# Cross-attention with layer norm: a new written order for the last ten tiles, head halves kept together, and three small changes at the end

## The chip, the core and the metric

The kernel runs on one core of one Trainium2 chip. The core has a matrix engine (TensorE, PE in the profile; its weight loads are the row PEld), a vector engine (VectorE, DVE), an activation engine (ScalarE, ACT), a general engine (GpSimd, POOL) and a queue engine (SyncE, SP). Each works through its own instructions in order; they meet by semaphores. DMA transfers are issued from SP, ACT or POOL and move data between the device memory (HBM), the on-chip buffer (SBUF) and within SBUF. Matmul results land in eight banks of an accumulation memory (PSUM) of 512 fp32 columns each. The metric is device time in microseconds (us), the median of several runs.

## The reference

There are 4 batches of 2048 rows of x, each row 512 wide, and 4 contexts of 77 rows. What is computed:

```python
qs = (x @ wq)                     # 16 heads of 32
ks, vs = ctx @ wk, ctx @ wv
scores = einsum(qs, ks) / sqrt(32)
scores = where(mask, -inf, scores)    # mask over the 77 keys
attn = softmax(scores) @ vs           # per head
out = attn @ wo + x
mu, var = mean(out), mean((out - mu)**2)   # over the 512 columns
return (out - mu) / sqrt(var + 1e-5) * gamma + beta
```

All inputs and outputs are fp32.

## The kernel before, in words

The 8192 rows are 64 tiles of 128 rows, numbered 0 to 63. Two tiles are a block (0 to 31), four a group that shares one load of x transposed, 16 a batch. To keep precision at the fast matmul rate, the big products (q projection, output projection) split each operand into a rounded high part and a low rest (both fp32r) and add three products: high by high, low by high, high by low. That is 12 matmuls of 128x128 weights and 512 columns for a projection of a tile.

One tile goes through these steps; the letters are the words in which the last ten tiles' order is written:

- `Q` / `q` (lines 173 to 189): a quarter of a group's q projection on TensorE, and its copy to SBUF by VectorE.
- `S` (L302): 64 small score matmuls into four banks, one for each head index j within groups of four.
- `T54.2` (L316): for quarter 2 of tile 54 (the four heads of one bank), VectorE adds the mask, writes the scores to a buffer `pbuf`, and finds the row maxima (negated). This frees the bank.
- `e` (L330): ScalarE's exponentials of a quarter, with row sums.
- `r`, `n` (L341, L346): VectorE's reciprocal of the 16 sums, then GpSimd's normalisation of the whole tile. For tile 63 alone, `h63.0`, `m63.0` and `h63.1`, `m63.1` do it in two halves (L354, L360).
- `t` (L370): VectorE transposes the tile in 32x32 blocks into buffer B.
- `P26.7s` (L382): piece 7 of the 12 DMAs which regroup block 26's transposed tiles into the tile PT; the last letter is the issuing queue (s SP, g POOL, a ACT). `U62.7s` is the same for a single tile, used for 62 and 63.
- `V` / `W` (L400, L415): attention times values, for a block (two banks) or for one of the last two tiles. `a`, `b` (or `c`, `d` for single tiles; L431, L435): ScalarE and VectorE split the result into high part AH and low part AL.
- `O` (L466): the output projection, 12 matmuls; in the last ten tiles the four that need AL come last. `x` loads the rows of x; `+` (L469) adds them on VectorE. `X` (L453) instead opens O's bank with the rows of x by one plain fp32 matmul with an identity matrix; then there is no `+`, and the statistics read PSUM.
- `s` (L505, L507): VectorE's mean and variance, or `I`, `J` (L513, L519): ScalarE's mean and squares. `u` (L529 to L532): GpSimd's 1/sqrt(var + eps), two small instructions. 
- `y` and `z` (L555, L558): VectorE's (o - mean) * gamma, then * rstd + beta. Or `k` (ScalarE's scaling, L541) or `p` (GpSimd's, L545), followed by `f`: GpSimd's times gamma, plus beta (L496, L497). `M0` and `M1` copy gamma and beta into two PSUM banks that stay taken, for y and z. `i`, `j`, `v` are a cast and split of x transposed, and a bias for k.
- `w` (L500): the store of the tile, issued on SP.

Tiles 0 to 53 are laid out by the loop at L644, two tiles a turn, with scores of later tiles, projections and norms of earlier ones interleaved. From S54 on (420.5 us in the profile) the order of all remaining work is the text `ORDER`, read word by word: a word puts its instructions at the end of their engines' queues, and every engine keeps that order. PSUM banks are given out in a ring of eight by the same order, so that a word that takes a bank waits for the last reader of what held it before.

Buffer `pbuf` has three slots, B two, PT two: T of tile t waits for t of tile t-3, t of a block for all P of the block two before, P for the V two blocks before.

## Time and profile before

| | us |
|---|---|
| median of 3 runs | 517.16 |
| lowest, highest | 516.73, 517.35 |
| the profiled execution: its time | 516.79 |
| the profiled execution: its span, first to last instruction | 515.0 |
| busy of the span: PE, DVE, ACT, POOL | 503.8, 473.5, 470.3, 418.7 |
| last matmul ends | 507.9 |
| last instruction of VectorE ends | 512.1 |

A timeline row reads: start, length, engine, line, operation, what it writes and from what, shape, how many in a row, and in square brackets how long the engine had been idle and what ended that. Lengths of neighbours overlap, because instructions are pipelined: the step from start to start is the price. The chain rows read start, length, what. A row of waits reads: who waited for whom, us in total, times, longest.

### The profile page before, as it was taken

Reading aid. Unit: us, or ns where it says so; the run is one execution under the profiler, and the core shown is the slowest. Engines: PE = TensorE matmul, PEld = TensorE weight load, DVE = VectorE, ACT = ScalarE, POOL = GpSimd, SP = SyncE. Lnnn points to the kernel's source line nnn. Section 1 sums busy time; section 2 is a strip of 40 time slices with the busy share of each in tenths; the row PEclk is TensorE's granted clock in tenths of the full one; section 3 lists DMA queues with packets and bytes.
Section 4 is the critical chain, followed back from the end, with each engine's and each line's share of the span. In section 5 each row is a group of like instructions: output and inputs, shape, how many; then the busy total and the mean of one; then the engine's idle time right before and its main releaser. Section 6 shows DMA issues by size and latency. Waiting matters only on the chain.

```text
span 515.0 us, 20430 instructions
## 1 busy us (share of the span) xinstructions
PE 503.8 (98%) x6836; PEld 385.2 (75%) x6836; DVE 473.5 (92%) x2572; ACT 470.3 (91%) x2240; POOL 418.7 (81%) x376
## 2 busy tenths in 40 slices
...
GB/s 319 396 138 162 208 187 178 227 200 206 228 214 208 231 211 229 215 205 202 212 206 224 234 218 214 203 198 223 227 193 229 200 207 233 183 222 176 175 210 209
DMA packets 58937, 110.24 MB, mean 214 GB/s; under 512 B 9393, under 2 KB 11313, under 8 KB 58833
## 3 DMA queue, kind: packets, MB, share of 16 engines
...
q8 instruction: 55, 0.90, 0.8%
...
q14 instruction: 50, 0.40, 0.2%
...
## 4 chain that ended last, share of the span: by engine, by line
PE 83%; DMA 5%; POOL 4%; DVE 4%; SPq 2%; issue 1%; ACT 0%; DVEq 0%; POOLq 0%
PE pq L170 30%; PE po L466 29%; PE sc L302 10%; PE pa L400 10%; DMA PT<-B 4%; SPq L382 2%; PE pv L236 2%; DVE B L370 1%; PE pk L196 1%; PE pq L599 1%; POOL mvt L532 1%; DVE pbuf L316 1%; POOL o_end L545 1%; DMA xtf<-xT 1%; POOL o_end L496 1%
## 5 line engine op out<-in xcount | busy, mean ns | idle before, releaser
L330 ACT ACTIVATE pbuf<-pbuf,nm 128x77 f32<-128x77 f32 x1024 | 352.5, 352 | 16.2 <-DVE nm L316 14.8
L330 ACT ACTIVATION_READ_ACCUMULATOR pbuf<-pbuf,nm 128x1 f32 x1024 | 196.9, 192 | 0.0
L316 DVE CUSTOM_DVE_ANT_0 pbuf<-sc,mb 128x77 f32<-128x77 f32 x1024 | 170.7, 230 | 23.3 <-PE sc L302 23.2
L346 POOL TENSOR_TENSOR pbuf<-pbuf,ri 128x1232 f32<-128x1232 f32 x63 | 142.2, 2258 | 22.9 <-DVE ri L341 16.1
L170 PE MATMUL pq<-xth,wqh 128*128 128x512 f32 (+1 forms) x256 | 98.8, 386 | 0.0
L170 PE MATMUL pq<-xtl,wqh 128*128 128x512 f32 (+1 forms) x256 | 97.9, 382 | 0.0
L170 PE MATMUL pq<-xth,wql 128*128 128x512 f32 (+1 forms) x256 | 97.9, 382 | 0.0
L370 DVE STREAM_TRANSPOSE B<-pbuf 128x1280 f32<-128x1280 f32 x64 | 95.5, 1493 | 2.2 <-DMA PT<-B 1.8
L466 PE MATMUL po<-woh,AH 128*128 128x512 f32 x232 | 96.9, 418 | 0.0
L466 PE MATMUL po<-wol,AH 128*128 128x512 f32 x232 | 90.6, 391 | 0.0
L466 PE MATMUL po<-woh,AL 128*128 128x512 f32 x232 | 88.9, 391 | 0.0
L316 DVE DVE_READ_ACCUMULATOR2_ANT nm<- 128x1 f32 x1024 | 84.0, 82 | 0.0
L496 POOL TENSOR_TENSOR o<-o,gam 128x512 f32<-128x512 f32 x50 | 65.6, 1311 | 14.1 <-ACT o L492 14.0
L302 PEld LDWEIGHTS sc<-kct,q 32*64 32x64 f32 x4096 | 51.6, 130 | 24.4 <-issue 23.0
L497 POOL TENSOR_TENSOR o<-o,bet 128x512 f32<-128x512 f32 x50 | 64.5, 1289 | 3.9
L163 POOL TENSOR_TENSOR xtl<-xtf,xth 128x1024 fp32r<-128x1024 f32 x28 | 67.1, 2397 | 0.0
L302 PE MATMUL sc<-kct,q 32*64 32x77 f32 x4096 | 62.1, 237 | 0.7 <-DVE nm L316 0.3
L400 PE MATMUL pa<-PT,vsb 96*32 96x256 f32 x960 | 58.0, 382 | 1.5 <-DMA PT<-B 1.2
L170 PEld LDWEIGHTS pq<-xth,wqh 128*128 128x128 f32 x256 | 48.1, 188 | 9.8
L170 PEld LDWEIGHTS pq<-xth,wql 128*128 128x128 f32 x256 | 48.1, 188 | 9.4
L170 PEld LDWEIGHTS pq<-xtl,wqh 128*128 128x128 f32 x256 | 48.1, 188 | 9.1
L466 PEld LDWEIGHTS po<-woh,AH 128*128 128x128 f32 x232 | 43.5, 187 | 13.0 <-issue 0.7
...
## 6 DMA issues: line engine op xcount, KB each, us to landing
...
```

The costliest lines, as they stand in the source:

```text
L163: nc.gpsimd.tensor_tensor(l, fx.pop((g, c)), h.bitcast(F32), ALU.subtract)
L170: nc.tensor.matmul(pq, w[:, c, m * P : (m + 1) * P], r[:, c, rs], start=(n == 0), stop=(n == 11))
L236: nc.tensor.matmul(pv, ctx_s[c][i][:, r, :], v[c], start=(n == 0), stop=(n == 11))
L302: nc.tensor.matmul(sc[j][half : half + P // 2, g * NK : (g + 1) * NK], qs[q, g, r0 : r0 + P // 2], kct[q, g, t // TPB, keys_of(j)], start= ...
L316: nc.vector.tensor_tensor_reduce(pb[:, h // 2, (h % 2) * NK : (h % 2 + 1) * NK], scs[t][j][:, g * NK : (g + 1) * NK], mb[:, t % TPB, keys_ ...
L330: nc.scalar.activation(pb[:, h // 2, (h % 2) * NK : (h % 2 + 1) * NK], pb[:, h // 2, (h % 2) * NK : (h % 2 + 1) * NK], AF.Exp, bias=nmax[t ...
L346: nc.gpsimd.tensor_tensor(pv, pv, rv.to_broadcast((P, NP, 2, NK)), ALU.mult)
L370: nc.vector.transpose(bt.rearrange("p c q r -> p q c r"), pbuf[t % NPB].rearrange("p q (c r) -> p q c r", c=5),)
L400: nc.tensor.matmul(pas[b, g // 2][HD * j : HD * (j + 1), (g % 2) * BLK : (g % 2 + 1) * BLK], vsb[:, 2 * b // TPB, HD * h : HD * (h + 1)], ...
L466: nc.tensor.matmul(pos[t], a[:, c, rs], w[:, c, :], start=(first and n == 0), stop=(n == 11))
L496: nc.gpsimd.tensor_tensor(o, o, gam, ALU.mult)
L497: nc.gpsimd.tensor_tensor(o, o, bet, ALU.add)
```

## The change

It has five parts.

1. `ORDER` is written anew. Of its 398 words most are the same as before, in another sequence; some issues change their queue, and some tiles change the engines that normalise them: tile 59 and 61 get `x` and `+` in place of `X`; the words p and f now work on tiles 46 to 49, 51 and 53; tiles 55, 58 and 60 get their statistics by I and J; and tiles 52 and 56 are scaled by the words y, K (ScalarE times rstd) and G (GpSimd plus beta).
2. `slot(h)`: in pbuf and all that follows from it, the heads with j = 0, 1 of each group come first (slots 0 to 7), then those with j = 2, 3. Before, both halves alternated in pairs. The half views become plain halves.
3. `X` of tiles 62 and 63 takes the rows from the transposed group that is on the chip for the q projection: for each of four column pieces, two matmuls (high part, low part) with the transposed rows as weights and the identity as the 128 moving columns. Their loads x62 and x63 go.
4. O63 is computed in two column halves of 256, with 12 matmuls each; its statistics are taken per half and joined.
5. z63 is two half instructions, each followed by a store of its half, one issued on SP, one on ACT.

```diff
@@ -37,30 +37,32 @@
 KSCALE = 1.0 / HD**0.5
 LATE = 48
 CUT = 27
+HALVES = [slice(0, D // 2), slice(D // 2, D)]
 ORDER = """
-i31 S54 Q59 T54.2 e54.2 x50 k46 T54.1 j31 T54.0 x56 q58 T54.3 S55 x59 O49 q59 e54.1 e54.3 T55.1 T55.0 T55.2 t53
-e54.0 e55.1 S56 r54 P26.7g Q61 x61 x58 k47 T55.3 e55.3 V25 P26.2s T56.3 n54 x51 T56.0 e55.0 +49 x57 P26.3s e55.2 f46
-P26.4s T56.1 T56.2 q61 S57 a25.0 t54 r55 n55 T57.0 e56.1 P26.9s T57.1 b25.0 s49 P26.1g w46 Q63 T57.2 P26.0s O48
-a25.1 b25.1 S58 e56.0 t55 e56.3 P27.8s e56.2 Q62 T57.3 q63 P26.6g e57.2 Q60 P26.10g e57.0 f47 r56 P26.8s e57.1 T58.2
-P26.11s T58.3 T58.1 T58.0 P26.5g P27.1s x52 x60 +48 P27.7g e57.3 P27.3s e58.3 n56 P27.0g e58.1 S59 P27.10g q62 t56
-r57 s48 V26 q60 e58.2 T59.0 a26.1 T59.1 S60 e58.0 P27.2g T59.2 P27.11g O51 n57 t57 e59.2 T59.3 P27.5g a26.0 e59.3
-O50 T60.1 x53 P27.9s T60.3 r58 T60.0 +51 b26.1 e59.0 b26.0 P27.4s e59.1 T60.2 P27.6s e60.0 P28.6s P28.2g S61 P28.10s
-u48 e60.2 P28.3s n58 t58 P28.1s +50 r59 T61.2 V27 T61.1 x54 P28.11s P28.7s T61.0 T61.3 O53 P28.4s e60.3 P28.8g n59
-t59 w47 S62 P28.0g a27.1 b27.1 O52 P29.6g e60.1 a27.0 T62.2 s51 b27.0 e61.0 e61.3 P28.5s e61.1 P29.8g P28.9s T62.1
-P29.2g r60 n60 O54 +53 T62.0 s50 S63 e61.2 T62.3 t60 e62.1 e62.3 P29.0g +52 u50 u51 x55 r61 T63.2 e62.0 O55 n61
-T63.0 P29.3s e62.2 +55 T63.1 P29.9s P29.7s t61 V28 +54 P29.4s P29.10s P29.5s T63.3 p50 a28.0 b28.0 a28.1 P29.11s M0
-r62 P29.1s x62 P30.3s e63.3 f50 s55 P30.2s P30.1s V29 P30.10s P30.7g n62 b28.1 y55 P30.9s a29.0 v51 a29.1 P30.5s X59
-P30.6s b29.0 P30.4s s54 O56 I52 P30.11s P30.8s t62 e63.0 e63.1 y48 e63.2 P30.0g U62.7s u54 b29.1 k51 u55 h63.0 w50
-O57 m63.0 +56 h63.1 I56 U62.9s U62.3s O59 U62.11s U62.6s U62.0g s53 y52 U62.8s U62.2s V30 m63.1 J52 M1 x63 a30.0 s59
-t63 y59 U62.5a +57 U62.4a U63.9a J56 O58 y49 U63.3s U63.8s U63.10s z55 U62.1g b30.0 u49 a30.1 f51 X62 U63.2a U63.5s
-b30.1 X61 U63.6s O60 u56 U63.1a y54 U63.0s z48 O61 w55 u53 U63.11s u52 z49 z54 U63.4a I57 y53 +58 U62.10a u59 p56
-J57 I61 W62 z53 U63.7s f56 w51 +60 s58 u57 W63 z52 w48 u58 s60 z59 u60 X63 y60 w49 c62 w56 J61 y57 d62 w52 c63 d63
-w59 w54 w53 z60 u61 O62 z57 w60 O63 p58 f58 y61 I62 z61 J62 w57 y62 u62 w58 s63 z62 w61 y63 u63 z63 w62 w63
+S54 i31 T54.0 Q59 q58 T54.3 x51 T54.2 e54.0 S55 T54.1 x57 O49 q59 T55.0 e54.3 T55.1 j31 t53 e54.1 e54.2 r54 e55.0
+S56 P26.7g k46 O48 T55.2 +49 T55.3 T56.3 n54 V25 T56.1 T56.2 P26.5g +48 x59 e55.1 e55.3 P26.10s f46 x52 T56.0 e55.2
+x53 t54 e56.3 S57 r55 T57.3 a25.0 T57.1 Q62 T57.0 b25.0 a25.1 P26.2s b25.1 s49 n55 x50 T57.2 P26.8g Q61 P26.3g S58
+e56.2 P26.11s O51 x56 P26.0s t55 s48 u49 q62 e57.3 w46 Q63 P26.4g e56.0 T58.3 e56.1 e57.0 P26.6g p49 P27.7s u48
+P26.9s r56 q61 P26.1s P27.5g e57.1 P27.6s T58.2 T58.0 n56 k47 e57.2 +51 P27.8s T58.1 V26 e58.0 P27.2g r57 s51 S59
+q63 t56 Q60 n57 e58.3 P27.11s T59.0 T59.1 e58.1 x54 T59.2 e59.0 u51 p51 f47 t57 q60 a26.1 a26.0 b26.0 e58.2 P27.10s
+x61 b26.1 O50 P27.1s P27.9s S60 T59.3 P27.0s P27.4s e59.2 P28.5g P28.8s e59.1 e59.3 +50 O53 r58 T60.3 P28.3g P27.3s
+T60.0 S61 e60.0 T60.2 T60.1 P28.9s P28.2s n58 t58 e60.2 P28.0s e60.3 r59 +53 p48 P28.11s T61.0 x58 n59 P28.4s T61.1
+P28.10s e60.1 P28.7s P28.6s P28.1s T61.3 V27 a27.0 T61.2 f48 w47 t59 r60 P29.2s O52 P29.8s S62 +52 a27.1 e61.1
+P29.0s b27.0 P29.5s b27.1 s53 P29.10s T62.2 O54 T62.3 e61.2 n60 e61.3 P29.6g P29.9s e61.0 V28 e62.2 T62.1 T62.0
+P29.4s f51 +54 P29.11s a28.0 P29.7s S63 a28.1 e62.3 r61 t60 b28.0 P29.1s b28.1 n61 t61 P29.3s f49 T63.2 T63.0 e62.0
+T63.3 e62.1 e63.2 O55 O57 r62 x55 u53 T63.1 +55 P30.7s P30.4s V29 P30.2s O56 e63.1 P30.8g a29.0 P30.10g s50 M0 s52
+P30.9g n62 +57 P30.11g P30.6s b29.0 t62 u52 P30.0s P30.5s a29.1 b29.1 P30.3s P30.1a e63.0 O59 +56 U62.6s U62.3s
+h63.0 e63.3 s54 I56 h63.1 w51 U62.11s U62.2s +59 O58 U62.5a m63.0 I55 s59 J56 x60 m63.1 v53 J55 y50 t63 V30 u50 M1
+U62.7g U62.4s a30.1 y54 X63 U63.10g U62.0s y52 U62.9s U62.1s u56 U63.11g U63.9s b30.1 +58 U63.1s X62 y59 a30.0
+U63.2s I58 U63.6g U63.3g w49 I57 b30.0 U63.0s z50 y55 y56 J58 U63.4s u54 u59 u55 U63.7g K52 k53 U63.5s z59 O60 K56
+z54 U62.8s J57 u58 U62.10s U63.8s +60 O61 W62 w59 I60 y58 w48 c62 G52 y57 z55 +61 J60 W63 G56 y60 w52 d62 w50 u57
+u60 w56 O62 c63 I61 w54 f53 d63 z57 J61 w55 z60 u61 y61 O63 w57 I62 w60 z58 y62 z61 J62 u62 w53 s63 u63 z62 w58 y63
+w61 w62 z63 w63
 """
@@ -120,7 +122,9 @@
     ident = const.tile([P, D // 2], F32, name="ident")
     warm = ident.bitcast(BF16)
     ident = ident[:, :P]
+    unit = ident.bitcast(F32R)
     mhalf, mneg, gates = small[:, 0:2], small[:, 2:4], small[:, 4:5]
+    last_st = small[:, 8:20].rearrange("p (n s) -> p n s", n=2)
     pbuf = [const.tile([P, NP, PW], F32, name=f"pbuf{i}") for i in range(NPB)]
     vm = small[:NK2, 64:128].rearrange("p (a r) -> p a r", a=2)
@@ -140,6 +144,10 @@
     def split(hi, lo, src):
         nc.scalar.copy(hi, src)
         nc.vector.tensor_tensor(lo, src, hi.bitcast(F32), ALU.subtract)
+
+    def slot(h):
+        g, j = divmod(h, GH)
+        return 2 * (NG * (j // 2) + g) + j % 2
     def keys_of(h):
         return slice(TAIL_K, NK2) if h % 2 == 0 else slice(0, NK)
@@ -313,27 +321,24 @@
         nm = nmax[t]
         for h in HEADS[lo:hi]:
             g, j = divmod(h, GH)
+            i = slot(h)
             nc.vector.tensor_tensor_reduce(
-                pb[:, h // 2, (h % 2) * NK : (h % 2 + 1) * NK],
+                pb[:, i // 2, (i % 2) * NK : (i % 2 + 1) * NK],
                 scs[t][j][:, g * NK : (g + 1) * NK],
                 mb[:, t % TPB, keys_of(h)],
                 -1.0,
                 3.0e38,
                 ALU.add,
                 ALU.min,
-                accum_out=nm[:, h : h + 1],
+                accum_out=nm[:, i : i + 1],
             )
     def exps(t, lo, hi):
         pb = pbuf[t % NPB]
-        for h in HEADS[lo:hi]:
+        for i in map(slot, HEADS[lo:hi]):
+            p = pb[:, i // 2, (i % 2) * NK : (i % 2 + 1) * NK]
             nc.scalar.activation(
-                pb[:, h // 2, (h % 2) * NK : (h % 2 + 1) * NK],
-                pb[:, h // 2, (h % 2) * NK : (h % 2 + 1) * NK],
-                AF.Exp,
-                bias=nmax[t][:, h : h + 1],
-                scale=-1.0,
-                accum_out=sums[t][:, h : h + 1],
+                p, p, AF.Exp, bias=nmax[t][:, i : i + 1], scale=-1.0, accum_out=sums[t][:, i : i + 1]
             )
     def recip(t):
@@ -346,7 +351,7 @@
         nc.gpsimd.tensor_tensor(pv, pv, rv.to_broadcast((P, NP, 2, NK)), ALU.mult)
     def half_view(ap, r):
-        return ap.rearrange("p (g r a) -> p g r a", r=2, a=2)[:, :, r]
+        return ap[:, r * H // 2 : (r + 1) * H // 2]
     def recip_half(t, r):
         if t not in ris:
@@ -354,9 +359,8 @@
         nc.vector.reciprocal(half_view(ris[t], r), half_view(sums[t], r))
     def normalise_half(t, r):
-        pv = pbuf[t % NPB].rearrange("p (g r) w -> p g r w", r=2)[:, :, r, : 2 * NK]
-        pv = pv.rearrange("p g (a k) -> p g a k", a=2)
-        rv = half_view(ris[t], r)[:, :, :, None]
+        pv = pbuf[t % NPB][:, r * NG : (r + 1) * NG, : 2 * NK].rearrange("p q (a k) -> p q a k", a=2)
+        rv = half_view(ris[t], r).rearrange("p (q a) -> p q a", a=2)[:, :, :, None]
         nc.gpsimd.tensor_tensor(pv, pv, rv.to_broadcast((P, NG, 2, NK)), ALU.mult)
     def transp(t):
@@ -400,7 +404,7 @@
                 nc.tensor.matmul(
                     pas[b, g // 2][HD * j : HD * (j + 1), (g % 2) * BLK : (g % 2 + 1) * BLK],
                     vsb[:, 2 * b // TPB, HD * h : HD * (h + 1)],
-                    pt[:NK2, :, h % 2, h // 2].rearrange("p i t r -> p t i r"),
+                    pt[:NK2, :, h % 2, slot(h) // 2].rearrange("p i t r -> p t i r"),
                     start=True,
                     stop=True,
                 )
@@ -415,7 +419,7 @@
                 nc.tensor.matmul(
                     pas[b, tt][HD * j : HD * (j + 1), g * P : (g + 1) * P],
                     vsb[:, t // TPB, HD * h : HD * (h + 1)],
-                    pt[:NK2, :, h % 2, tt, h // 2],
+                    pt[:NK2, :, h % 2, tt, slot(h) // 2],
                     start=True,
                     stop=True,
                 )
@@ -435,7 +439,7 @@
         nc.vector.tensor_tensor(at_part(b, 1, i, by_tile)[0], pv, hv.bitcast(F32), ALU.subtract)
-    def load_x(t):
+    def place(t):
         if t < NT - 8:
             od[t] = sb.tile([P, D], F32, tag="o", bufs=8, name=f"o_{t}")
         elif t < NT - 4:
@@ -446,11 +450,21 @@
             if t // 2 not in ends:
                 ends[t // 2] = sb.tile([P, 2, GRP], F32, tag="xtf", name=f"o_end_{t}")
             od[t] = ends[t // 2][:, t % 2]
+
+    def load_x(t):
+        place(t)
         nc.sync.dma_start(od[t], x[t * P : (t + 1) * P, :])
     def resid(t):
         pos[t] = bank(f"po_{t}")
-        nc.tensor.matmul(pos[t], ident, od[t], start=True, stop=False)
+        if t < NT - 4:
+            nc.tensor.matmul(pos[t], ident, od[t], start=True, stop=False)
+            return
+        place(t)
+        for c in range(NC_D):
+            for n, part in enumerate(gx[t // 4]):
+                rows_t = part[:, c, t % 4 * P : (t % 4 + 1) * P]
+                nc.tensor.matmul(pos[t][:, c * P : (c + 1) * P], rows_t, unit, start=(c == 0 and n == 0), stop=False)
     def o_proj(t):
         b, tt = divmod(t, 2)
@@ -462,8 +476,12 @@
         prods = [(n == 2, c, a, w) for c in range(NC_D) for n, (a, w) in enumerate(((ah, woh), (ah, wol), (al, woh)))]
         if t >= 2 * CUT:
             prods.sort(key=lambda p: p[0])
-        for n, (_, c, a, w) in enumerate(prods):
-            nc.tensor.matmul(pos[t], a[:, c, rs], w[:, c, :], start=(first and n == 0), stop=(n == 11))
+        halves = [slice(0, D)] if t < NT - 1 else HALVES
+        for cols in halves:
+            for n, (_, c, a, w) in enumerate(prods):
+                go = first and n == 0 and cols.start == 0
+                done = n == 11 and cols.stop == D
+                nc.tensor.matmul(pos[t][:, cols], a[:, c, rs], w[:, c, cols], start=go, stop=done)
     def residual(t):
         nc.vector.tensor_tensor(od[t], pos.pop(t), od[t], ALU.add)
@@ -501,8 +519,13 @@
     def moments_one(t):
-        st = sb.tile([P, 6], F32, tag="st", bufs=3, name=f"st_{t}")
-        nc.vector.bn_stats(st, pos.get(t, od[t]))
+        if t < NT - 1:
+            st = sb.tile([P, 6], F32, tag="st", bufs=3, name=f"st_{t}")
+            nc.vector.bn_stats(st, pos.get(t, od[t]))
+        else:
+            st = last_st
+            for n, cols in enumerate(HALVES):
+                nc.vector.bn_stats(st[:, n], pos.get(t, od[t])[:, cols])
         mvs[t, 1] = sb.tile([P, 4], F32, tag="mvt", bufs=64 - LATE, name=f"mvt_{t}")
         nc.vector.bn_aggr(mvs[t, 1][:, :2], st)
@@ -553,6 +576,12 @@
     def centre(t):
         row = gam if t in pos else rows.get(0, gam)
         nc.vector.scalar_tensor_tensor(od[t], pos.pop(t, od[t]), mvs[t, 1][:, 0:1], row, ALU.subtract, ALU.mult)
+
+    def finish_last(t):
+        for cols, queue in zip(HALVES, (nc.sync, nc.scalar)):
+            o = od[t][:, cols]
+            nc.vector.scalar_tensor_tensor(o, o, mvs[t, 1][:, 2:3], rows.get(1, bet)[:, cols], ALU.mult, ALU.add)
+            queue.dma_start(out[t * P : (t + 1) * P, cols], o)
     def finish(t):
         nc.vector.scalar_tensor_tensor(od[t], od[t], mvs[t, 1][:, 2:3], rows.get(1, bet), ALU.mult, ALU.add)
@@ -699,7 +728,7 @@
         if u == 0:
             load_wo()
             nc.gpsimd.memset(ident, 0.0)
-            nc.gpsimd.affine_select(ident, ident, [[-1, P]], ALU.not_equal, 1.0, base=0, channel_multiplier=1)
+            nc.gpsimd.affine_select(unit, unit, [[-1, P]], ALU.not_equal, 1.0, base=0, channel_multiplier=1)
         if k == TPB - 6 and m + 1 < NB:
             load_mask(m + 1)
         if k == TPB - 4 and m + 1 < NB:
@@ -774,6 +803,10 @@
     def do(op, k, part=0, queue="s"):
         if op == "k" and k >= LATE:
             scale_one(k)
+        elif op == "z" and k == NT - 1:
+            finish_last(k)
+        elif op == "w" and k == NT - 1:
+            od.pop(k)
         elif op in tile_ops:
             tile_ops[op](k)
         elif op in tile_parts:
```

## The prediction

> **What bounds the kernel now.** I read the page first, then the busy time of four stretches, the waits of TensorE in the stage that changes, and the chain of the last ten microseconds.
>
> ```profile
> span 515.0 us, 20430 instructions
> PE 503.8 (98%) x6836; PEld 385.2 (75%) x6836; DVE 473.5 (92%) x2572; ACT 470.3 (91%) x2240; POOL 418.7 (81%) x376
> ```
>
> The stretches (length, then busy time of PE, PEld, DVE, ACT and POOL, PE clock, DMA share, GB/s):
>
> ```profile
> 420.00:455.00 35.00, 34.33 (x613) 26.12 (x612) 33.40 (x237) 34.91 (x187) 27.82 (x29) 1.00 0.81 207
> 455.00:485.00 30.00, 29.71 (x379) 21.97 (x378) 28.84 (x146) 29.19 (x157) 23.51 (x26) 1.00 0.74 192
> 485.00:508.00 23.00, 22.59 (x171) 16.01 (x169) 22.45 (x40) 10.08 (x26) 21.22 (x30) 1.00 0.67 219
> 508.00:515.00 7.00, 0.00 (x0) 0.00 (x0) 2.94 (x5) 0.00 (x0) 2.42 (x5) 0.82 0.39 150
> ```
>
> The written order begins at 420.5. From there to 508 TensorE, VectorE and (until the last exponential, 485.0) ScalarE all run without a visible hole; from 485 GpSimd replaces ScalarE as the third full queue. The last 7 us hold no matmul at all. What TensorE waits for from 420 on is small:
>
> ```profile
> PE sc L302 <- DVE nm L316: 0.3, 1, 0.3
> PE pa L400 <- DMA PT<-B: 0.3, 1, 0.3
> PE pa L400 <- DMA o<-x: 0.3, 1, 0.3
> PE sc L466 <- DVE AL L435: 0.3, 1, 0.3
> ```
>
> So the tail is worth changing in two places only: the sum of TensorE's work, and the stretch behind its last matmul. That stretch, on VectorE and in the chain:
>
> ```profile
> 507.90 0.70 DVE L505 BATCH_NORM_STATS2 st<-sc 128x6 f32<-128x512 f32 x1
> 508.63 0.18 DVE L507 BATCH_NORM_AGGREGATE mvt<-st 128x2 f32<-128x6 f32 x1
> 509.83 0.75 DVE L558 SCALAR_TENSOR_TENSOR o_end<-o_end,mvt,sc 128x512 f32<-128x512 f32 x1 [1.02 <-POOL mvt L532]
> 510.50 0.74 DVE L555 SCALAR_TENSOR_TENSOR o_end<-sc,mvt,gam 128x512 f32<-128x512 f32 x1
> 511.35 0.75 DVE L558 SCALAR_TENSOR_TENSOR o_end<-o_end,mvt,sc 128x512 f32<-128x512 f32 x1
> ```
>
> ```profile
> 504.11 2.09 POOL o_end L545
> 506.27 1.31 POOL o_end L496
> 507.65 1.26 POOL o_end L497
> 508.91 0.26 POOL mvt L529
> 509.24 0.57 POOL mvt L532
> ```
>
> z62 waited 1.02 us for u62, which stood on GpSimd behind p58 and f58 (504.11 to 508.91). From z63's end (512.10) to the end of the span are 2.9 us: the last store.
>
> **The change, part by part.** The TensorE rows that price it:
>
> ```profile
> 8.03 0.64 PE L599 MATMUL pq<-xth,wqh 128*128 128x256 f32 x4
> 8.51 0.64 PE L599 MATMUL pq<-xtl,wqh 128*128 128x256 f32 x4
> 450.01 0.73 PE L302 MATMUL sc<-kct,q 32*64 32x77 f32 x6
> 451.06 0.89 PE L302 MATMUL sc<-kct,q 32*64 32x77 f32 x58 [0.32 <-DVE nm L316]
> 481.27 0.39 PE L466 MATMUL po<-woh,AH 128*128 128x512 f32 x1
> 483.99 0.39 PE L466 MATMUL sc<-woh,AH 128*128 128x512 f32 x1
> 491.52 1.88 PE L453 MATMUL sc<-o_end,ident 128*128 128x512 f32 x4
> 493.46 0.40 PE L466 MATMUL po<-wol,AH 128*128 128x512 f32 x1
> 506.79 1.07 PE L466 MATMUL sc<-woh,AL 128*128 128x512 f32 x4
> ```
>
> *Residuals.* O57's first matmul is at 481.27 and the next tile's, twelve on, at 483.99: 0.227 us each. X62 and X61 lie from 491.52 to O60's second matmul at 493.46, less one such step: 1.71, 0.855 us each. Four X of this kind go: -3.42. Two come back as eight matmuls of 128 columns each. No row has that shape. Above it lies the 512-column step (0.227, so 1.82 per X); the nearest is the 256-column one with equal weights, four in 0.48 us (8.03 to 8.51), 0.12 each. I take 0.12: 0.96 per X, +1.92 for two. They need no load, so x62 and x63 leave SP.
>
> *Who carries the normalisation.* Against before, VectorE gets two + (0.6 each) and loses two s (0.9 each: 507.90 to 508.81) and two z (0.67): -1.9. It is 22.45 of 23 us busy before the end, so this matters: it must reach s63 by 506.5, and its queue sum (below) gives 503.8 with waits left out, some 2.5 us of cover; with none, its lateness would be the end's. ScalarE gets two I and J pairs and two K, about 5 us, into a stretch where it is busy 10.08 of 23: hidden.
>
> Below 0.12 the trace has no such row. The Trainium skill (TensorE: Matmul & The Clock Gate, Back-to-back issue gap) gives 81 ns sustained for 128 columns, an estimate of 0.65 per X and 0.6 us less in all; but it gives 131 ns for 512, where this trace has 227, so I don't build on it.
>
> *The last projection in column halves.* 24 matmuls of 256 columns at 0.12 for twelve at 0.227: 2.88 - 2.72 = +0.16. TensorE's own work: -3.42 + 1.92 + 0.16 = -1.34, so its end goes from 507.86 (506.79 + 1.07) to 506.5.
>
> *Behind it.* Only the second half's statistics are left (about half of 0.70, 0.36, plus start and aggregate, 0.22): 0.58. z62 then follows at once if u62 is done, 0.67 (509.83 to 510.50), y63 0.66, z63 in two halves of 0.40 (half of 0.75, a little over), and 2.90 for the store: 5.61 for 7.14, -1.53. u63 (0.90 by the chain's 0.26, 0.57 and a gap) fits under z62 and y63 (1.33). What made u62 late is gone: p56, f56, p58, f58 (4.7 us each pair) are no longer at the end; GpSimd's last long items are G52, G56 and f53, the last followed by u61, u62, u63. Queue sums put f53's end near 503.5. I take nothing for two smaller stores on two queues.
>
> On that last point the Trainium skill (DMA: Bandwidth & Descriptors, Anatomy of one DMA) has about 2.0 us fixed and bytes over 436 GB/s: half of 256 KB would save an estimated 0.3 us and no more. No run here shows a half-size store.
>
> *The order itself.* Matmuls, exponentials (40 quarters), transposes and projections are the same in number. S60 was stretched from 0.95 to 1.94 us (450.01 to 451.95): its banks come free with T59.0 and T59.1, and VectorE had lost time here:
>
> ```profile
> 446.66 1.51 DVE L370 STREAM_TRANSPOSE B<-pbuf 128x1280 f32<-128x1280 f32 x1 [1.43 <-DMA PT<-B]
> ```
>
> For queue sums I add up durations in the written order from 420.5, waits left out (a T is four scans, a t one transpose):
>
> ```profile
> L316 DVE CUSTOM_DVE_ANT_0 pbuf<-sc,mb 128x77 f32<-128x77 f32 x1024 | 170.7, 230 | 23.3 <-PE sc L302 23.2
> ```
>
> By them (four scans of 170.7/1024 make 0.67, a t 1.45) S60 came 0.2 us after T59.1 before and comes 5 us after it now; -1.0 if nothing replaces it. What is late next: V26 moves up from a queue sum of 447.8 to 446.9, while P26.9 and P26.1 stand on SP behind P27.7, which waits for t55. They would be issued by about 442.6 and land at 445 to 447. A late V26 costs TensorE all of its lateness. I take the order at 0, with -1.0 and +1.5 as ends.
>
> *GpSimd before n62.* p48, p49, p51, f48, f49, f51 and their u move from the end to here.
>
> ```profile
> 425.33 2.41 POOL L163 TENSOR_TENSOR xtl<-xtf,xth 128x1024 fp32r<-128x1024 f32 x1
> 450.59 0.57 POOL L382 DMA_DIRECT2D PT<-B  x1
> 480.00 2.27 POOL L346 TENSOR_TENSOR pbuf<-pbuf,ri 128x1232 f32<-128x1232 f32 x1
> ```
>
> Before, 425.33 to 480.00 held j31 2.4, eight n 18.1, three f 7.9, one p 2.1, three u 2.5 and 19 DMA issues 10.8: 43.8 of 54.7 us. Now: 2.4 + 18.1 + five f 13.2 + three p 6.3 + four u 3.4 + 14 issues 8.0 = 51.4. Slack falls from 11 to 3 us. It costs nothing while each n ends before its t is due: by the sums n58 ends at 457.9 against t58 at 458.0, n62 at 479.7 against t62 at 480.4. That cover is thin; gone, each microsecond of a late t62 is one of a late t63.
>
> *Halves of heads.* e63.3 now comes after h63.0, so the first half is normalised under the last exponentials, and only m63.1 is left behind them.
>
> ```profile
> 485.00 0.82 ACT L541 ACTIVATE o<-o,mvt 128x512 f32<-128x512 f32 x1
> 487.40 1.24 POOL L360 TENSOR_TENSOR pbuf<-pbuf,ri 128x616 f32<-128x616 f32 x1
> 488.67 1.51 DVE L370 STREAM_TRANSPOSE B<-pbuf 128x1280 f32<-128x1280 f32 x1 [0.31 <-POOL pbuf L360]
> 490.44 4.64 SPq L382 DMA_DIRECT2D PT<-B  x6
> 495.77 1.23 SPq L382 DMA_DIRECT2D PT<-B  x2
> DMA to landing us min/median/max: 2.1/2.5/3.2
> ```
>
> Before, m63.1 began 2.4 us after the exponentials (485.0). Now it may end at 486.5; but +59, s59 and y50 (2.1 us) stand between h63.1 and t63, so t63 starts near 487.3, 1.4 earlier, ending near 488.8. Ten issues follow on SP (seven U63, w49, U62.8, U62.10) at 0.62 to 0.77: through at 495.0 to 496.5, landed 2.1 to 3.2 later, 497.1 to 499.7. W63 is due at 506.5 less O63 2.9, O62 2.9 and itself 1.0: 499.7. So this path gives nothing to the sum and just holds. On GpSimd U63.10g now waits for t63 (about 1 us), with u56, u54, u59 and u55 behind it; z59, the first to need one of these, stands eight VectorE items (some 5.5 us) after t63, and u59 is done 4.6 us after it: covered by 1 us, at most a small loss on VectorE.
>
> **Sum.** -1.34 - 1.53 = -2.87 on a span of 515.0. The profiled execution took 516.79, 0.37 under the median 517.16; from the median, 514.3 us.
>
> **Rivals.**
> 1. *128 columns cost as much as 512.* +1.72: 516.0. For it: no row under 256 columns with full weights. Against: 256 costs half of 512.
> 2. *GpSimd paces the middle.* If t62 comes 2 us late through p and f ahead of the n's, t63, U63 and W63 slip alike: 516.3. For it: 3 us slack. Against: the queue sums, just.
> 3. *The other side: tile 63's pieces land late.* Place: TensorE in front of W63. Once the last U63 lands after 499.7, each microsecond is lost whole, since only O62 and O63 are left; from 502.6 on (2.9 late) the kernel is slower than before. For it: SP issues of this kind took 0.77 each at 490 to 495, and t63 hangs on O59 through +59, on GpSimd and on ScalarE. 4.5 us late gives 518.8. Against: t63 should be earlier.
> 4. *The order buys nothing:* new waits of V26 to V30 eat all of it, 517.2. For it: DMA share 0.81 from 420 to 455.
>
> **How the numbers follow.** The likeliest case 0.50 (its own range 512.7 to 515.8: half-store and S60 below, V26 above), rival 1 0.12, rival 2 0.10, rival 3 0.19, rival 4 0.09. 0.2% is 1.0 us, about what the runs can tell from no change (they spread 0.6): faster means under 516.1. Faster: 0.50, rival 1 0.12 and most of rival 2, 0.70. Same: 0.11. Slower: rival 3, 0.19. Range 512.7 to 517.6, which leaves out the worse part of rival 3 and a little below.
>
> **What would show it.** Last matmul near 506.5; sixteen residual matmuls taking under 2.2 us; no wait of z62 on GpSimd; two half stores issued about 2.7 us after the last matmul; t63 starting near 487. Wrong if TensorE shows a wait of over 1 us before V26 to V30, W62 or W63, or if t58 or t62 wait for GpSimd.

## The result, and the profile after

The changed kernel takes 514.53 us at the median (512.40 to 518.05), beside 516.80 for the kernel before on the same chip (515.50 to 519.68). The ratio is 0.9946, with a 95% interval of 0.9924 to 0.9968: 0.5% faster. The prediction was 514.3, worked out from a median of 517.16; against 516.80 the change gains 2.27, where 2.87 was forecast. The profiled execution took 513.36 us, its span is 511.2. The page, in the form shown of before:

```profile
span 511.2 us, 20463 instructions
PE 501.9 (98%) x6856; PEld 385.4 (75%) x6856; DVE 472.1 (92%) x2570; ACT 473.7 (93%) x2250; POOL 420.9 (82%) x377
```

TensorE is 1.9 us shorter, VectorE 1.4; ScalarE has 3.4 us more. What TensorE waits for from 419 us on (in us: total, times, longest):

```profile
PE po L419 <- DMA PT<-B: 0.7, 1, 0.7
PE pa L404 <- issue: 0.2, 1, 0.2
```

Of the four waits of before, S60's, V26's and O62's are gone; V27 still waits 0.2 (0.3 before), and one new wait of 0.7 has come, in front of W62. The profile puts V27's wait down to `issue`, that is to nothing it can name. V26, S60, the first and last of the new residual matmuls, O60's first, W62 with W63, and the first matmul of each of the last tile's halves, on TensorE's timeline (start, length):

```profile
445.80 1.93 PE L404 MATMUL pa<-PT,vsb 96*32 96x256 f32 x32
454.20 0.95 PE L310 MATMUL sc<-kct,q 32*64 32x77 f32 x64
488.35 0.33 PE L467 MATMUL pa<-ident,xth 128*128 128x128 f32 x1
490.08 0.27 PE L467 MATMUL po<-ident,xtl 128*128 128x128 f32 x1
490.19 0.45 PE L484 MATMUL sc<-woh,AH 128*128 128x512 f32 x1
496.58 2.15 PE L419 MATMUL po<-PT,vsb 96*32 96x128 f32 x64 [0.71 <-DMA PT<-B]
501.54 0.28 PE L484 MATMUL pa<-woh,AH 128*128 128x256 f32 x1
502.98 0.28 PE L484 MATMUL pa<-woh,AH 128*128 128x256 f32 x1
```

S60 takes 0.95 in one piece, where it took 1.94. Sixteen residual matmuls of 128 columns lie between 488.35 and 490.19, 0.115 each (0.112 from start to start inside the two tiles), 0.92 us per tile. The halves of tile 63 begin at 501.54 and 502.98; the last matmul ends at 504.57. Behind it, on VectorE:

```profile
504.21 0.74 DVE L587 SCALAR_TENSOR_TENSOR o_end<-o_end,mvt,pa 128x512 f32<-128x512 f32 x1
504.87 0.76 DVE L528 BATCH_NORM_STATS2 small<-pa 128x6 f32<-128x256 f32 x2
505.66 0.21 DVE L530 BATCH_NORM_AGGREGATE mvt<-small 128x2 f32<-128x12 f32 x1
506.17 0.75 DVE L587 SCALAR_TENSOR_TENSOR o_end<-o_end,mvt,pa 128x512 f32<-128x512 f32 x1 [0.31 <-POOL mvt L555]
506.84 0.74 DVE L578 SCALAR_TENSOR_TENSOR o_end<-pa,mvt,gam 128x512 f32<-128x512 f32 x1
507.69 0.87 DVE L583 SCALAR_TENSOR_TENSOR o_end<-o_end,mvt,pa 128x256 f32<-128x256 f32 x2
```

Both half scans (L528) begin 0.30 after the last matmul, behind z61; z62 still waits 0.31 for u62 on GpSimd; z63 begins 3.12 after the last matmul.

Runs of one kernel spread by several us, and much of that lies ahead of the changed order: the first score matmul of tile 54 began anywhere from 418.99 to 422.58 us in the profiled executions below. So I compare the profiles from that matmul on, and call this stretch the tail: first score matmul of tile 54 to the end of the span. All figures are differences of rows of the trace, in us.

| run | tail | to the last matmul's end | from there to VectorE's end | from there to the span's end |
|---|---|---|---|---|
| before | 94.47 | 87.32 | 4.24 | 2.91 |
| after | 91.80 | 85.15 | 3.98 | 2.67 |
| after, repeated | 91.38 | 84.75 | 3.96 | 2.68 |
| before, GpSimd relieved | 93.95 | 87.61 | 3.43 | 2.91 |
| before, two residuals fewer | 94.78 | 88.51 | 3.34 | 2.93 |
| before, last tile in halves | 96.19 | 88.22 | 4.21 | 3.75 |
| the same, tile 62's store first | 94.83 | 87.52 | 4.21 | 3.10 |
| after, without halves | 91.42 | 84.38 | 4.05 | 2.99 |
| after, old form of residual | 91.97 | 84.97 | 3.98 | 3.03 |
| after, old head slots | 91.27 | 84.60 | 3.99 | 2.68 |
| after, two loads on ScalarE | 90.95 | 84.30 | 3.98 | 2.67 |
| and z62 on ScalarE, GpSimd | 90.75 | 84.29 | 3.79 | 2.68 |
| or z61 there | 90.42 | 84.31 | 3.27 | 2.84 |
| and tile 63 in two banks | 90.40 | 84.51 | 3.06 | 2.83 |

The repetition puts the uncertainty of a tail at 0.4 us at least; the kernel before has one profile only. By these profiles the change gains 2.7 to 3.1: 2.2 to 2.6 ahead of the last matmul's end, 0.5 behind it. The medians, 2.27 here and 2.14 in the repetition, say less.

### The profile page after: what moved, and what is told of

It is laid out like the page before. It is cut to its first block, busy times and chain, and to the rows that moved or that the text cites. A ratio compares the mean times of both kernels' runs of the same rounds, so it can differ in the third digit from the quotient of the medians.

```text
span 511.2 us, 20463 instructions
## 1 busy us (share of the span) xinstructions
PE 501.9 (98%) x6856; PEld 385.4 (75%) x6856; DVE 472.1 (92%) x2570; ACT 473.7 (93%) x2250; POOL 420.9 (82%) x377
## 4 chain that ended last, share of the span: by engine, by line
PE 89%; SPq 4%; DMA 2%; DVE 2%; issue 1%; POOL 1%; ACT 0%; DVEq 0%
PE pq L178 33%; PE po L484 31%; PE sc L310 11%; PE pa L404 10%; SPq L386 3%; PE pv L244 2%; PE pk L204 1%; DMA stage_a<-wq 1%; PE pq L628 1%; DMA o<-x 1%; DVE o_end L578 1%; POOL pbuf L351 0%; DVE o_end L587 0%; DMA PT<-B 0%; SPq L456 0%
## 5 line engine op out<-in xcount | busy, mean ns | idle before, releaser
L484 PE MATMUL po<-woh,AH 128*128 128x512 f32 x236 | 98.5, 417 | 0.0
L484 PE MATMUL po<-wol,AH 128*128 128x512 f32 x236 | 92.3, 391 | 0.0
L514 POOL TENSOR_TENSOR o<-o,gam 128x512 f32<-128x512 f32 x52 | 68.1, 1310 | 14.4 <-ACT o L510 14.3
L515 POOL TENSOR_TENSOR o<-o,bet 128x512 f32<-128x512 f32 x52 | 67.0, 1289 | 4.1
```

The lines of the kernel that those rows point to most:

```text
L484: nc.tensor.matmul(pos[t][:, cols], a[:, c, rs], w[:, c, cols], start=go, stop=done)
L514: nc.gpsimd.tensor_tensor(o, o, gam, ALU.mult)
L515: nc.gpsimd.tensor_tensor(o, o, bet, ALU.add)
```

## The experiments

One remark holds for all. In the order before, the squares (J) of tile 52, and in the changed order those of tile 62, stand behind the step y that centres the tile and multiplies it by gamma in place, so they are taken of the scaled values. The reference takes the variance ahead of gamma, so this one tile's rstd is not the reference's; with gamma drawn with a spread of 0.2 around one, it is off by an estimated 3 to 4%. Whoever uses the order should put J ahead of y, as the last three kernels do for tile 62.

**The changed kernel again.** No edit.

> The changed kernel once more, for a second profile of it. From the first score matmul of tile 54 to the end of the span it took 91.8 us in the first profile, against 94.5 before; what came ahead of tile 54 took 419.4 against 420.5, in code that differs only in where head pieces lie in a buffer. If the 1.1 us ahead of tile 54 belongs to the change, the second profile shows it again (419.0 to 419.8); if it is scatter between executions, tile 54 may start anywhere from 419 to 421.5, and the tail is again 91.5 to 92.2 us.

Measured: 514.10 us, ratio 0.9944 (0.9921 to 0.9968). Tile 54 began at 421.20, so the early 419.43 of the first profile was scatter. The wait in front of W62 is 0.12 here, not 0.71, and the tail is shorter by 0.4. The gain stands; the wait varies.

**One part alone: GpSimd relieved.** Kernel before, with tile 58 finished by ScalarE instead of GpSimd's p58:

```diff
- z57 w60 O63 p58 f58 y61
+ z57 w60 O63 v58 k58 f58 y61
```

> The kernel before, with one tile's scaling taken off GpSimd's last stretch: tile 58 is scaled by ScalarE (v58, k58) instead of GpSimd (p58, 2.08 us). Nothing else moves. My theory (in the order before, u62 behind p58 and f58 sets the end): u62 starts about 1.0 to 1.6 us earlier, the 1.02 us wait of z62 for GpSimd is gone or under 0.2 us, and from the last matmul to the end of the span it takes 6.1 to 6.3 us instead of 7.14; the last matmul stays where it was. Rival (the end is set by VectorE's queue alone): 7.1 us as before.

Measured: 515.67 us, ratio 0.9984 (0.9970 to 0.9998). On VectorE:

```profile
508.51 0.75 DVE L558 SCALAR_TENSOR_TENSOR o_end<-o_end,mvt,sc 128x512 f32<-128x512 f32 x1 [0.22 <-POOL mvt L532]
```

z62's wait fell from 1.02 to 0.22, and 0.8 us went from behind the last matmul. From the last matmul to the span's end it takes 6.34, close to the expected 6.1 to 6.3. So u62's place on GpSimd was a real price of the old order, and a separate one; the tail shows 0.5 of it, since the last matmul came 0.3 later in this profile.

**One part alone: two residuals fewer on TensorE.** Kernel before without X59 and X61; VectorE adds them (+59, +61).

```diff
- ... a29.1 P30.5s X59
+ ... a29.1 P30.5s
- x63 a30.0 s59
+ x63 a30.0 +59 s59
- b30.1 X61 U63.6s O60
+ b30.1 U63.6s O60
- J57 I61 W62 z53 U63.7s f56 w51 +60 s58
+ J57 W62 z53 U63.7s f56 w51 +60 +61 I61 s58
```

> The kernel before, with X59 and X61 taken out and +59 and +61 put in on VectorE, as the new order has it; the rest of the old order stays. If TensorE's sum alone set the end, the last matmul and the end would both come 1.7 us earlier. My theory: the last matmul comes 0.5 to 1.7 us earlier (VectorE, 22.45 of 23 us busy, takes two more instructions of 0.65 us each and may hold back AL for O62 and O63), but the end moves by less than 0.5 us, because u62 still stands behind p58 and f58 on GpSimd, whose queue did not change. Rival (VectorE becomes the bound): the last matmul not earlier, the end 0.5 to 1.3 us later.

Measured: 515.86 us, ratio 0.9987 (0.9957 to 1.0016): no gain that can be told, though TensorE has 1.7 us less to do. TensorE's waits from 420 on:

```profile
PE sc L466 <- DVE AL L435: 1.4, 1, 1.4
PE sc L466 <- ACT AH L431: 0.6, 1, 0.6
```

O62 now waits 2.0 us for the high and low parts (AH, AL) that it multiplies, and the last matmul comes 1.2 later after tile 54's first, not 0.5 to 1.7 earlier: the rival holds there. In the old order VectorE stands right behind TensorE. That the changed kernel could take its residuals off TensorE because it also took two z and two s off VectorE is argued from this; no run tested it.

**One part alone: the last tile in halves.** Kernel before with the halves of O63, s63 and z63 and the two half stores, as in the change.

> The kernel before, with the last tile in column halves alone (projection, statistics, z63 and its two stores); old order, old residuals. My theory: TensorE's end 0.16 us later; the statistics behind it 0.35 us shorter, but hidden under the wait for u62, which stays at 508.9 on GpSimd; z63's first half stored 0.4 us earlier, the second no earlier: the end moves by -0.3 to +0.2 us. Rival (the halves are worth what they save by themselves, as if nothing else stood at the end): -0.5 to -0.9 us.

Measured: 517.75 us, ratio 1.0026 (1.0008 to 1.0045): slightly slower. z62 still waited for GpSimd, 0.78, and from VectorE's end to the span's end it took 0.84 longer, where -0.3 to +0.2 was expected. On SP:

```profile
514.53 0.33 SPq L572 DMA_DIRECT2D out<-o_end  x1
514.92 0.42 SPq L506 DMA_DIRECT2D out<-o_end  x1
```

The half stores are issued within z63, and in the old order w62 stands behind z63: tile 62's 256 KB store (L506) is now issued last, behind the first half (L572). To test that, w62 was moved:

```diff
- z63 w62 w63
+ w62 z63 w63
```

> The kernel before with the last tile in halves, as in the run that was 0.26% slower, but with tile 62's store issued ahead of tile 63's last step, not behind its two half stores. Theory (0.8 us of that loss was SP issuing 62's 256 KB last): from VectorE's last instruction to the end 2.7 to 2.9 against 3.75, first score matmul of tile 54 to the end 95.2 to 95.4 against 96.19 and 94.47 before: still no gain over the kernel before, the time 516.9. Rival (the half stores themselves are slow to land): 3.7 again, 517.7.

Measured: 515.95 us, ratio 1.0026 (0.9997 to 1.0055). From VectorE's end to the span's 3.10, not 3.75: the place of w62 was the larger part of the loss there, by 0.65. The expected 2.7 to 2.9 was missed; tile 62's store now goes out right ahead of the two halves, but that this delays them was not tested. No gain over the kernel before can be told either way: in that order the halves are worth nothing that these runs show.

**One part undone: no halves.** The changed kernel with tile 63 whole.

```diff
- halves = [slice(0, D)] if t < NT - 1 else HALVES
+ halves = [slice(0, D)]
```

(and s63, z63 and w63 as for the other tiles)

> The changed kernel with its last tile whole again (projection, statistics, z63, one store). In two profiles of the changed kernel the tail, from tile 54's first score matmul to the end of the span, took 91.8 and 91.4 us, and s63 began 0.3 us after the last matmul because VectorE still had z61, so the first half's statistics never ran under the second half's matmuls. Theory A (the prediction's term): the halves save 0.35 on the statistics and 0.35 on z63, so without them the tail is 92.1 to 92.4. Theory B (from the profiles): two half scans take 0.76 for 0.70 and the matmuls 0.16 more, so only the earlier store of the first half is left: tail 91.3 to 91.9 without them.

Measured: 514.65 us, ratio 0.9972 (0.9942 to 1.0003); the tail is 91.42, between the two of the changed kernel. Behind the last matmul the whole tile takes 7.04, the halves 6.64 to 6.65: 0.4 gained there. Ahead of it, with W62's wait taken off (85.15 - 0.71, 84.75 - 0.12, and 84.38 - 0.06 without halves), the halves take 84.44 and 84.63 against 84.32: 0.1 to 0.3 lost. The halves are worth 0.1 to 0.3 at best, within what a tail can tell.

**One part undone: the form of the residual.** X62 and X63 as one 512-column matmul each of the loaded tile against the identity; x62 and x63 come back on SP.

> The changed kernel with X62 and X63 as before: loads of their rows (issued behind P30.3 on SP, where it stood idle for 3 us) and one plain fp32 matmul with the identity each. The profile showed the new form at 0.11 us per matmul, 0.90 per tile, against 0.855 for the old. My theory: the form is worth nothing by itself; TensorE's time from tile 54 to its last matmul (85.1 and 84.8 in two profiles) and the tail (91.8, 91.4) stay within 0.4 us. Rival (the saved loads matter): tail longer by 0.6 us or more, with a wait of TensorE before V30 or W62 for regrouping transfers.

Measured: 514.68 us, ratio 0.9968 (0.9927 to 1.0010), tail 91.97, W62's wait 0.65. No difference that a tail can tell: TensorE takes 0.92 us per tile in the new form and 0.855 in the old, and the two loads on SP made no new wait of TensorE.

**One part undone: the head slots.** The changed order, with the two halves of heads interleaved in the buffer as before.

```diff
- g, j = divmod(h, GH)
- return 2 * (NG * (j // 2) + g) + j % 2
+ return h
```

> The changed kernel with the heads where they were (both halves alternating in pairs), in the new order. If the tracking of reads and writes covers a strided half by its whole range, m63.0 has to wait for e63.3 as well. Theory A (the prediction: the first half is normalised under the last exponentials): t63 begins 0.8 to 1.4 us later than the 486.06 - 419.43 = 66.6 us after tile 54's start, and the tail grows by up to 1 us. Theory B (from the profile: m63.0 began at 483.06, 0.6 us after e63.3's end, behind h63.0, and t63 stood behind VectorE's +59, s59, y50): no change, t63 at 66.4 to 66.9, tail 91.2 to 92.0.

Measured: 512.89 us, ratio 0.9950 (0.9922 to 0.9978), tail 91.27. t63 begins 66.63 us after the first score matmul of tile 54 (487.20 less 420.57), in the changed kernel also 66.63 (486.06 less 419.43). Putting the halves together in the buffer buys nothing; t63 is held by VectorE. Nor was the first half normalised under the last exponentials, as the prediction has it: ScalarE's last one ends at 482.48, and GpSimd stood idle for 1.52 until VectorE had done the first half's reciprocal. In the changed kernel, GpSimd, then VectorE:

```profile
483.06 2.40 POOL L364 TENSOR_TENSOR pbuf<-pbuf,ri 128x616 f32<-128x616 f32 x2 [1.52 <-DVE ri L359]
```

```profile
483.88 0.69 DVE L487 TENSOR_TENSOR o_end<-sc,o_end 128x512 f32<-128x512 f32 x1
484.60 0.69 DVE L524 BATCH_NORM_STATS2 st<-o_end 128x6 f32<-128x512 f32 x1
485.33 0.18 DVE L530 BATCH_NORM_AGGREGATE mvt<-st 128x2 f32<-128x6 f32 x1
485.43 0.72 DVE L578 SCALAR_TENSOR_TENSOR o<-o,mvt,row 128x512 f32<-128x512 f32 x1
486.06 1.50 DVE L374 STREAM_TRANSPOSE B<-pbuf 128x1280 f32<-128x1280 f32 x1
```

There is no idle time between +59, s59, y50 and t63.

**A wait taken away: W62.** In the changed kernel the chain of work that ends last runs through SP's issues, of which this stretch is the end (start, length):

```profile
491.90 0.59 SPq L386
492.53 0.60 SPq L386
493.18 0.59 SPq L386
493.82 0.59 SPq L386
494.41 0.04 issue
494.45 2.00 DMA PT<-B
496.45 0.14 issue
496.58 1.11 PE po L419 x32
```

SP issues without a break at 0.59 each; U62.10 is the last of them for tile 62. ScalarE stands idle for 1.95 behind M1, until V30's result at 488.49, so U62.8 and U62.10 were given to its queue right behind M1:

```diff
- t63 V30 u50 M1
+ t63 V30 u50 M1 U62.8a U62.10a
- z54 U62.8s J57 u58 U62.10s U63.8s +60
+ z54 J57 u58 U63.8s +60
```

> The changed kernel with two of tile 62's pieces (U62.8, U62.10) issued on ScalarE's queue behind M1, where it idled for 1.95 us, instead of on SP, where they came 18th and 19th of 21 issues in one row. Theory A (SP's row of issues sets W62: the chain runs through it, and TensorE waited 0.71 and 0.12 us there): no wait of TensorE before W62, y60's wait on VectorE (0.94 and 0.34) under 0.2, tail 90.8 to 91.4. Theory B (the wait is another transfer's): a wait of the same size remains, tail 91.4 to 91.8.

Measured: 513.88 us, ratio 0.9940 (0.9911 to 0.9969). TensorE has no visible wait in front of W62 any more; the 0.2 in front of V27 stays. VectorE's wait in front of y60, which hangs on W62 by way of ScalarE, is 0.17, and was 0.9. The tail is 90.95, the last matmul 84.30 behind tile 54's first. So the row of issues on SP was the cause of W62's wait.

**Taking the work away that stands behind the last matmul.** On top of that edit, J62 moved ahead of y62 and tile 62 finished by ScalarE (K62) and GpSimd (G62) instead of z62:

```diff
- I62 w60 z58 y62 z61 J62 u62 w53 s63 u63 z62 w58 y63
+ I62 J62 w60 z58 y62 z61 u62 K62 G62 w53 s63 u63 w58 y63
```

> The changed kernel with TensorE's two late weight loads of unit 62 issued by ScalarE, tile 62's squares taken straight after its sum (of the projection's own output, where the changed kernel takes them of the centred and scaled tile), and tile 62's last step taken off VectorE: ScalarE stretches it, GpSimd adds the last row. Theory (VectorE's queue of tile 61's and 62's steps and the wait for GpSimd's 62 are what ate the halves' gain): the 0.31 wait and the 0.67 step are gone from VectorE, but GpSimd's 1.30 for tile 62 now stands ahead of its two steps for tile 63, so from the last matmul to VectorE's last instruction 3.4 to 3.5 us against 3.98, first score matmul of tile 54 to the end 90.3 to 90.6, the time 513.3. Rival (the end of tile 63 is a chain of its own, with VectorE's earlier steps in its shadow): 3.98 and 90.9 as in the run with the two loads alone, 513.9.

Measured: 513.65 us, ratio 0.9938 (0.9916 to 0.9961). Tail 90.75, and 3.79 from the last matmul to VectorE's end: 0.2 gained instead of 0.5. On GpSimd:

```profile
505.22 0.27 POOL L552 TENSOR_SCALAR mvt<-mvt,nz 128x1 f32<-128x1 f32 x1
505.58 0.55 POOL L555 TENSOR_TENSOR mvt<-mvt,small 128x1 f32<-128x1 f32 x1
506.96 1.26 POOL L574 TENSOR_TENSOR o_end<-o_end,bet 128x512 f32<-128x512 f32 x1 [0.83 <-ACT o_end L571]
508.18 0.19 POOL L554 TENSOR_TENSOR mvt<-mvt,nz 128x1 f32<-128x1 f32 x1
508.45 0.55 POOL L555 TENSOR_TENSOR mvt<-mvt,small 128x1 f32<-128x1 f32 x1
```

u62 came at 505.22 behind f53 and u61, so G62 stood in front of u63, and z63 waited 0.79 for that. My figure had left out f53. The second kernel gives tile 61 to ScalarE and GpSimd instead, and lets VectorE do z62 while GpSimd does u63:

```diff
- I62 J62 w60 z58 y62 z61 u62 K62 G62 w53 s63 u63 w58 y63
+ I62 J62 w60 z58 y62 u62 K61 G61 w53 s63 u63 w58 y63 z62
```

> As the run beside it, but the tile that ScalarE and GpSimd finish is 61, and VectorE finishes 62 while it would wait for GpSimd's steps of tile 63. So VectorE is free when the first half of tile 63 is done. Theory (the halves are worth what was predicted once VectorE is free at that point): the first half's statistics begin ahead of the last matmul's end; behind it stand 0.4 of the second half, 0.2, GpSimd's 0.9 and the last step's 0.87, about 2.6 us against 3.98, and the tail is 89.6, the time 512.6. Rival (GpSimd's 1.30 for tile 61 comes late and stands ahead of its steps for 63): 3.4, the tail 90.4, no better than the run beside it.

Measured: 512.45 us, ratio 0.9918 (0.9890 to 0.9947). Tail 90.42, and 3.27 from the last matmul to VectorE's end. Neither mechanism holds, though the rival's figures (3.4 and 90.4) are near. GpSimd is no longer waited for, but TensorE, then VectorE:

```profile
503.90 0.28 PE L484 MATMUL pa<-woh,AH 128*128 128x256 f32 x1
504.86 0.64 PE L484 MATMUL pa<-woh,AL 128*128 128x256 f32 x4
```

```profile
504.52 0.75 DVE L578 SCALAR_TENSOR_TENSOR o_end<-po,mvt,gam 128x512 f32<-128x512 f32 x1
505.53 0.76 DVE L528 BATCH_NORM_STATS2 small<-pa 128x6 f32<-128x256 f32 x2 [0.26 <-PE pa L484]
506.33 0.21 DVE L530 BATCH_NORM_AGGREGATE mvt<-small 128x2 f32<-128x12 f32 x1
```

VectorE was free 0.26 before it began, the first half of tile 63 was summed more than 1 us earlier (the second half's matmuls begin at 503.90), and yet both scans begin 0.03 after the last matmul's end (504.86 + 0.64).

**Two banks.** So the last kernel puts the second half's sum, with the residual of its columns, in tile 60's PSUM bank, which VectorE has read long before, and centres the halves one by one. With that, the first half's sum is also marked as ended (`stop`) by its own last matmul; before, only the second half's last matmul carried the mark. In part:

```diff
+ if cols.start:
+     to = pos[t, 1] = ring[-4]
+     rows_in(t, range(NC_D // 2, NC_D), to)
...
- nc.tensor.matmul(pos[t][:, cols], a[:, c, rs], w[:, c, cols], start=go, stop=done)
+ nc.tensor.matmul(to[:, cols], a[:, c, rs], w[:, c, cols], start=first and n == 0, stop=n == 11)
...
- nc.vector.bn_stats(st[:, n], pos.get(t, od[t])[:, cols])
+ nc.vector.bn_stats(st[:, n], (pos[t, 1] if n else pos[t])[:, cols])
```

> As the run that finishes tile 61 on ScalarE and GpSimd, but the second half of tile 63 is summed in another PSUM bank (tile 60's, read long before), the residual of its columns going there just ahead of it, and the centring of tile 63 is done in two halves. In that run VectorE was free 0.26 before the last matmul ended and yet began the first half's statistics 0.03 after it. Theory (the scan of the first half waits for the end of the second, since both lie in one bank): with two banks the first scan begins when VectorE is free, about 0.3 before the last matmul's end; the second follows it, 0.38 less behind the last matmul, and the halved centring costs 0.13, so 3.0 us from the last matmul to VectorE's last instruction against 3.27. Rival (it waited for TensorE's queue as such, not for the bank): the first scan still begins behind the last matmul, 3.4 us.

Measured: 511.93 us, ratio 0.9918 (0.9896 to 0.9939). TensorE, then VectorE:

```profile
503.85 0.33 PE L491 MATMUL sc<-woh,AH 128*128 128x256 f32 x1
504.85 0.64 PE L491 MATMUL sc<-woh,AL 128*128 128x256 f32 x4
```

```profile
504.75 0.42 DVE L535 BATCH_NORM_STATS2 small<-pa 128x6 f32<-128x256 f32 x1
505.52 0.43 DVE L535 BATCH_NORM_STATS2 small<-sc 128x6 f32<-128x256 f32 x1 [0.36 <-PE sc L491]
505.99 0.21 DVE L537 BATCH_NORM_AGGREGATE mvt<-small 128x2 f32<-128x12 f32 x1
506.24 0.48 DVE L590 SCALAR_TENSOR_TENSOR o_end<-pa,mvt,gam 128x256 f32<-128x256 f32 x1
506.64 0.47 DVE L590 SCALAR_TENSOR_TENSOR o_end<-sc,mvt,gam 128x256 f32<-128x256 f32 x1
```

Now the first scan (504.75 to 505.17) runs while the second half's matmuls are still running (to 505.49). Two things could have held it before: the shared bank, or the missing end mark. The score matmuls speak for the bank: there each matmul carries its own marks, and VectorE's first scan needs two of the 64, the first and the fifth. In the kernel before, VectorE stands idle, and yet:

```profile
308.56 0.95 PE L302 MATMUL sc<-kct,q 32*64 32x77 f32 x64
309.50 0.24 DVE L316 CUSTOM_DVE_ANT_0 pbuf<-sc,mb 128x77 f32<-128x77 f32 x1 [1.47 <-PE sc L302]
```

The scan begins as the last of the 64 ends (309.51), not 0.9 earlier. So here the reader waits for every matmul that stands ahead of it in the program and writes its bank. No run tells whether the chip or the program's own waits hold it, and none has two banks without the mark.

From the last matmul to VectorE's end it takes 3.06 instead of 3.27, as expected; 0.2 of TensorE's side (84.51 for 84.31) eats it in this profile, so the tail is the same. The median is the lowest of all, but the ratio is the one of the run before it (0.9918), so what the second bank adds to the time is not shown. That the three last edits together beat the changed kernel is supported by the tail (90.40 against 91.38 and 91.80); the interval of the ratio overlaps with that of the changed kernel's repetition (0.9921 to 0.9968).

## Why the prediction was right, and where not

The time was right (514.3, measured 514.53), and the sum fits the tails: -2.87 forecast, -2.67 and -3.09 measured. The medians gained 2.27 and 2.14, but the forecast started from a median 0.36 higher than the later one, and that closed part of the gap. Of the sum's two terms, one was too small and the other too large by about the same, so that the sum came out so near is luck.

*TensorE's own work: right.* Four old residuals went out, and two new ones came in at 0.92 (forecast 0.96, from the 256-column row). The halved projection takes 1.44 from the first half's first matmul to the second's, so 2.88 in all, as forecast. Rival 1, 128 columns at the price of 512, is excluded. The Trainium skill (TensorE: Matmul & The Clock Gate, Back-to-back issue gap) gives 81 ns for 128 columns, sustained; here it is 112 to 115 at a granted clock of 0.998, as it was 227 against its 131 at 512.

*The order, taken at 0: the term that was too small.* To the last matmul's end the tails are 2.17 and 2.57 shorter, where the work accounts for 1.34 by the forecast. With W62's waits of 0.71 and 0.12 taken off, 1.35 to 1.54 are left for the order: the end named as -1.0, S60's stretch, and the small waits of V26 and O62 (0.3 each) with it. The end named as +1.5, a late V26, did not come: V26 started at 445.80 without a wait. What is late next was therefore not V26 but W62, and the prediction had priced that place (ten pieces, landing "497.1 to 499.7") for W63 only, with U62.8 and U62.10 among the same ten issues but due for W62, which stands right ahead of W63 and takes 1.1. SP's queue never pauses there, so each issue ahead of U62.10 counts. Giving two issues to ScalarE removed the wait.

*Rival 4 and the two residuals.* The run with two residuals fewer shows that TensorE's work counts only where VectorE keeps up: in the old order 1.7 us of TensorE's work bought nothing, since VectorE was as late. The prediction's "it must reach s63 by 506.5" named the right place, but its "some 2.5 us of cover" was not there: VectorE reached s63 0.30 after the last matmul.

*Behind the last matmul: the term that was too large.* Forecast 5.61, measured 6.65, before 7.14. Piece by piece: the scans and the aggregate end 1.30 after the last matmul (505.87 less 504.57), not 0.58; z62's wait of 0.31 was forecast as none; y63 to z63 takes 0.85 from start to start, not 0.66 (before it was 0.85 too, 510.50 to 511.35: that row was at hand); z63's halves 0.87 for 0.80; the end 2.67 for 2.90. The two half stores were issued 3.6 and 4.0 after the last matmul, not "about 2.7 us". The step that failed is "Only the second half's statistics are left". In the changed kernel VectorE is late for it, but with VectorE free it fails still: both halves lie in one PSUM bank, and the first scan waits for the second half's matmuls. The Trainium skill (PSUM — Partial Sum Buffer, PSUM bank collisions raise a hardware error) says that two engines may not touch one bank in the same partitions at the same time, disjoint columns included, and that the compiler's back end orders such accesses. The traces agree with such an order: with one bank, 0.26 of waiting; with two banks, 0.42 of scan under matmuls. I had not weighed that rule in the prediction, and it speaks against this part of the change; the wait of the first score scan behind 64 matmuls, above, was in the trace of the kernel before.

*z62's wait.* "What made u62 late is gone" was half right. ScalarE's J62, then GpSimd's u62:

```profile
504.33 0.72 ACT L542 ACTIVATE junk<-o_end,mvt 128x512 f32<-128x512 f32 x1 [1.91 <-DVE o_end L578]
```

```profile
505.25 0.26 POOL L552 TENSOR_SCALAR mvt<-mvt,nz 128x1 f32<-128x1 f32 x1 [1.71 <-ACT junk L542]
```

GpSimd is clear of p58 and f58 and stands idle for 1.71. But u62 needs J62 too, and J62 waits on ScalarE for y62, which VectorE reaches late. That J62 needs y62 at all is the new order's doing, since it stands behind y62 there. The prediction followed one of the two things that u62 waits for.

*GpSimd before n62: thinner than said.* GpSimd, then VectorE:

```profile
477.89 2.27 POOL L351 TENSOR_TENSOR pbuf<-pbuf,ri 128x1232 f32<-128x1232 f32 x1
```

```profile
480.19 1.51 DVE L374 STREAM_TRANSPOSE B<-pbuf 128x1280 f32<-128x1280 f32 x1
```

n62 ends at 480.16 and t62 starts at 480.19. Tile 54 began 1.11 earlier in this profile than in the one that the forecast was made from, so on its scale these are 481.3 and 481.3 (forecast 479.7 and 480.4): t62 is now released by GpSimd, 0.9 late. VectorE had been free for some 0.1, so by the prediction's own sign ("if t58 or t62 wait for GpSimd") this is a miss, though a small one. Rival 2, 2 us late, did not come. Rival 3, late pieces in front of W63, did not come: t63 started at 486.06, on the same scale 487.2 (forecast 487.3), and only W62's 0.71 shows that this path is near.

*The half store.* The span ends 2.67 after VectorE's last instruction, with a whole store 2.91: 0.24 less. The Trainium skill (DMA: Bandwidth & Descriptors, Anatomy of one DMA — SWDGE (gpsimd) path) gave an estimated 0.3, by a fit for DMAs that GpSimd issues; these stores go out on SP and ACT, so the likeness tests nothing. Nor is the gain sure: with the old form of the residual, the same two half stores took 3.03. The forecast's own range reaches down to 512.7, 1.6 below 514.3; S60's 1.0 and this 0.3 make 1.3 of that, and no row stands for the rest.

What stays open: why the first score matmul of tile 54 starts up to 3.6 us apart in different executions, and how much of the order's 1.4 is S60's and how much the waits'. No run undid the order alone, so that the order gave the 1.4 is argued from the waits that are gone, and not shown.
